# Another table of places for the last three graphs of a four-layer GNN stack

## The chip, the cores and the metric

The kernel runs on one core of a Trainium2 chip, in one launch. The metric is the device time of that launch in microseconds (us). Times of a kernel are given as the median of several runs; a profile is one execution of its own, with its own time.

## The reference

32 graphs of 512 nodes with 256 features (fp32) and a dense 512x512 integer adjacency each go, one by one and without any exchange, through four layers. Each layer is `h = relu(layernorm(x))`, `x = x + layer(h)`:

```python
x = x + _L0_gnn_ref(h, adj, W, a_src, a_dst)   # attention, 4 heads, additive scores, masked by adj > 0, elu
x = x + _L1_gnn_ref(h, adj, W, a)              # attention, 1 head, softmax over the other axis, elu
x = x + _L2_gnn_ref(h, adj, a_0, a_1, a_2, a_3)# scores (h*a_k) h^T, chosen by the value of adj, softmax
x = x + _L3_gnn_ref(h, adj, Wqkv, ..., W2, b2) # a transformer layer: 8 heads of 32, masked by
                                               # adj > 0 either way or the diagonal, layer norm,
                                               # feed-forward 256 -> 1024 -> 256, layer norm
```

All arithmetic is fp32.

## The kernel before

**How it is built.** `quick_path` does not issue instructions as it goes. A class `Plan` records *jobs*: one instruction of VectorE (DVE) or ScalarE (ACT), one DMA issue of SyncE (SP), or a few matmuls of TensorE (PE) that belong together. For each graph `b` the functions `masks`, `layer0`, `layer1`, `layer2` and `layer3` record 529 jobs, always the same ones, numbered by `plan.at` from 0 to 528. When all are recorded, `Plan.carry_out` sorts the jobs of all graphs by their *place*, issues them in that order, and ties each engine's instructions together, so that every engine, PE, DVE, ACT and SP alike, carries out its jobs strictly in the order of places. All jobs are issued from one line per kind: line 215 for DVE and ACT, 236 for SP, 266 and 268 for PE.

**What a place is.** Line 156:

```python
place = self.number * ROUND + self.own.get(self.number, self.table)[self.at] if self.place is None else self.place
```

`ROUND` is 100000. `PLACES` (line 291) holds one number for each of the 529 jobs of a graph, and all graphs use it but six: `OWN` (line 334) holds tables of their own for graphs 0, 1, 2, 29, 30 and 31. A place is a rank and nothing else: no instruction waits for a time. As the numbers of `PLACES` reach from 0 to some 459000 and graphs are 100000 apart, jobs of four to five graphs stand mixed in each engine's order: while PE does the feed-forward of one graph, DVE works on the attention of the next and ACT on the one behind. In the tables of graphs 29 to 31 the numbers reach into the millions: these only order the jobs at the end, where no further graph follows.

**Buffers.** `carry_out` also hands out buffers in the order of places: tiles of a kind share numbered slots (9 `big`, 19 `mid`, 8 `half`, 8 PSUM banks), a new tile gets the slot that has been free for longest, and its first writer waits for the last users of the tile before. So another order also gives other slots.

**The steps that the prediction names.** In `layer3`, the transformer layer:
- attention, for each of two groups `g` of four heads and four blocks `j` of 128 keys: a PE job `ps_s` (four score products, 32 rows deep), four ACT exponentials into `p`, one DVE product of `p` (128x2048) with the mask `m3`, a PE job `ps_ct` (four products with `v`), and from the second block on a DVE addition into `acc`, the sum that the softmax divides by. `acc` goes through a PE job `ps_to`, once for each group; the one of group 1 is the "second `ps_to`".
- the round trip of `inv`: ACT copies `ps_to` to `to`; SP sends it to DRAM and back (`to_d`, `seen`) so that it lies across partitions; DVE takes the reciprocals (`turned`); SP sends them out and back again (`in_d`, `inv`); DVE multiplies them into `cT`. Each step needs the one before.
- `ps_wo` (8 products of 256 columns) needs `cT` of both groups; DVE adds the residual (`t`), takes the norm's statistics (`st`, `mv`), ACT and DVE make `rstd` and `shift`, ACT writes four rows of `n`, PE transposes them (`ps_t3`; `ps_t` in the profile), ACT makes `tT`.
- the feed-forward: 16 products `ps_f1` of 512 columns, each pair followed by an ACT relu, then 32 products `ps_f2` of 256 columns; DVE adds them into `u`, the second norm gives `y`, and SP sends it out. The profile calls both `ps_f`.

In `layer1`, PE's `ps_sp` turns a small tile, and a DMA out and back spreads it into `rows1`, from which DVE makes the four blocks of `p1` that `ps_o1` needs; `layer2` has scores `ps_e`, transpositions `ps_y` and products `ps_o2`, both `ps_o` in the profile.

An fp32 product is two PE records in the profile, a transposition one.

## Time and profile before

| | us |
|---|---|
| median of 3 runs | 3430.3 |
| lowest and highest of them | 3425.57, 3436.63 |
| the profiled execution's own time | 3424.86 |
| its span, first to last instruction | 3422.9 |
| PE's mean granted clock, share of full speed | 0.994 |
| busy: PE, PE weight load, DVE, ACT | 3340.2, 1975.5, 2820.1, 2115.6 |
| PE's last product of the last graph ends | 3409.8 |

The page divides the span by engine, by 40 slices, by groups of equal instructions and by the chain of work that ended last. Lines name the source line, the engine, the operation and the tiles (output <- inputs, buffer numbers left out, so that `p` stands for `p0`, `p1`, `p2` and `p3`). As all jobs come from lines 215, 236, 266 and 268, tiles tell them apart, not lines. The view of waits gives total, number and longest wait for each pair of waiting and releasing instruction. The view of stages gives busy time of each engine within a window, with PE's granted clock there, the DMA engines' busy share and GB/s.

### The profile page before, as it was taken

The numbers are of one execution on the slowest core, as the hardware profiler recorded it, in microseconds if no ns is written. First come the engines' busy times: TensorE is split into PE (matmuls) and PEld (weight loads), VectorE is DVE, ScalarE is ACT, GpSimd is POOL, SyncE is SP. The second block draws the span as 40 slices with busy tenths as digits, with TensorE's granted clock in tenths as the row PEclk, the third lists the DMA queues.
The fourth block names the chain that finished last, engine by engine and source line by source line (L and its number), as shares of the span: only waits on it lengthen the run. The fifth ranks groups of instructions, "written<-read, shape, count | busy, mean of one in ns | idle before, by whom it ended". The sixth has DMA issues, their size and how long they took to land.

```text
span 3422.9 us, 48320 instructions
## 1 busy us (share of the span) xinstructions
PE 3340.2 (98%) x17842; PEld 1975.5 (58%) x17842; DVE 2820.1 (82%) x5499; ACT 2115.6 (62%) x4801; POOL 11.1 (0%) x25
## 2 busy tenths in 40 slices
PE   6999999999999999999999999999999999999995
PEld 4555566555566555665655665655655655655563
DVE  6887888888888888888888888888988888877954
ACT  5756667556666556676556676556676566675652
POOL 1000000000000000000000000000000000000000
PEclk9999999999999999999999999999999999999997
DMA  5111110111111111111111111111111111110000
GB/s 165 41 47 55 51 51 27 53 49 54 51 40 36 56 46 57 51 35 40 56 46 57 50 35 39 57 46 57 51 47 39 54 37 53 43 33 30 17 10 20
DMA packets 161171, 161.16 MB, mean 47 GB/s; under 512 B 92576, under 2 KB 126880, under 8 KB 156832
## 3 DMA queue, kind: packets, MB, share of 16 engines
q1 hardware_dynamic: 158464, 153.00, 15.3%
q0 software_dynamic: 1216, 3.94, 0.4%
q8 instruction: 143, 2.34, 0.3%
q10 hardware_dynamic: 1248, 1.05, 0.1%
q14 instruction: 100, 0.82, 0.1%
HBM read 122.96 MB, written 18.22 MB: 41 GB/s over the span
## 4 chain that ended last, share of the span: by engine, by line
PE 85%; DVE 8%; DMA 4%; ACT 3%; issue 1%; DVEq 0%; SPq 0%; ACTq 0%
PE ps_f L268 25%; PE ps_o L268 11%; PE ps_s L268 7%; PE ps_qk L268 6%; PE ps_wh L268 5%; PE ps_ct L268 5%; PE ps_oT L268 5%; PE ps_t L266 4%; PE ps_e L268 4%; PE ps_wo L268 3%; DVE p L215 3%; PE ps_v L268 3%; PE ps_den L268 3%; DMA inv<-in_d 2%; DVE acc L215 2%; PE ps_to L268 1%
## 5 line engine op out<-in xcount | busy, mean ns | idle before, releaser
L215 DVE TENSOR_TENSOR p<-p,m 128x2048 f32<-128x2048 f32 x256 | 577.8, 2277 | 3.3 <-ACT p L215 3.2
L215 ACT ACTIVATE p<-ps_s 128x512 f32<-128x512 f32 x1024 | 555.3, 616 | 35.0 <-PE ps_s L268 33.7
L268 PE MATMUL ps_f<-ff_t,f 128*128 128x256 f32 x2048 | 470.9, 381 | 0.0
L268 PE MATMUL ps_f<-tT,ff_t 128*128 128x512 f32 x1024 | 467.1, 597 | 0.4 <-ACT tT L215 0.4
L268 PEld LDWEIGHTS ps_f<-ff_t,f 128*128 128x128 f32 x2048 | 378.4, 190 | 87.7 <-issue 32.6
L215 DVE SCALAR_TENSOR_TENSOR p<-rows,seen,mT 128x512 f32<-128x512 f32 x512 | 352.7, 744 | 32.6 <-PE ps_oT L268 20.6
L215 ACT ACTIVATE rstd<-mv,eps 128x4 f32<-128x4 f32 x192 | 56.5, 294 | 522.4 <-DVE mv L215 509.5
L215 ACT ACTIVATE h<-x,shift,rstd 128x256 f32<-128x256 f32 x512 | 283.1, 599 | 94.5 <-DVE shift L215 94.2
L268 PEld LDWEIGHTS ps_f<-tT,ff_t 128*128 128x128 f32 x1024 | 185.4, 191 | 196.2 <-issue 154.5
L215 DVE TENSOR_TENSOR acc<-acc,p 128x2048 f32<-128x2048 f32 x128 | 292.5, 2285 | 2.3
L268 PE MATMUL ps_s<-qk 32*128 32x512 f32 x2048 | 287.9, 633 | 1.4 <-ACT qk L215 1.2
L215 ACT ACTIVATE f<-ps_f,ff1b_c 128x512 f32<-128x512 f32 x256 | 168.1, 684 | 132.3 <-PE ps_f L268 129.4
L268 PE MATMUL ps_ct<-p,v 128*32 128x512 f32 x2048 | 247.8, 599 | 0.0
L268 PE MATMUL ps_o<-h,p 128*128 128x257 f32 x1024 | 245.6, 383 | 0.5 <-DVE p L215 0.4
L268 PE MATMUL ps_o<-wh,p 128*128 128x256 f32 x1024 | 242.9, 385 | 0.4 <-ACT wh L215 0.4
L268 PE MATMUL ps_oT<-p,wh 128*32 128x512 f32 x2048 | 240.6, 594 | 0.0
L268 PE MATMUL ps_qk<-h3T,wqkv_t 128*128 128x512 f32 x512 | 239.2, 599 | 0.0
L268 PEld LDWEIGHTS ps_o<-wh,p 128*128 128x128 f32 x1024 | 189.9, 190 | 77.0 <-issue 25.9
L268 PEld LDWEIGHTS ps_o<-h,p 128*128 128x128 f32 x1024 | 189.1, 190 | 52.5 <-PE ps_den L268 20.1
L266 PE MATMUL ps_t<-ident,h 128*128 128x128 f32 x1024 | 171.7, 278 | 32.7 <-ACT h L215 31.9
L215 DVE BATCH_NORM_STATS2 st<-x 128x6 f32<-128x256 f32 x512 | 197.6, 413 | 5.7 <-DMA x<-in_x_dram 0.7
L266 PEld LDWEIGHTS ps_t<-ident,h 128*128 128x128 f32 x1024 | 127.5, 142 | 114.3 <-issue 71.0
(135 smaller groups left out, 4928.7 us busy)
## 6 DMA issues: line engine op xcount, KB each, us to landing
adj<-in_adj_dram SPq DMA_DIRECT2D x32, 1024.0 KB
rows<-rows_d SPq DMA_DIRECT2D x32, 1024.0 KB
x<-in_x_dram SPq DMA_DIRECT2D x32, 512.0 KB
rows<-rows_d SPq DMA_DIRECT2D x32, 512.0 KB
inv<-in_d SPq DMA_DIRECT2D x64, 256.0 KB
out_dram<-y SPq DMA_DIRECT2D x32, 512.0 KB
mT<-m SPq DMA_TRANSPOSE x128
ff_t<-in_L_gnn_W_dram POOLq DMA_DIRECT2D x2, 1024.0 KB, 10.3
```

The lines of the kernel that those rows point to most:

```text
L215: return [getattr(unit, method)(*map(real, args), **{k: real(v) for k, v in kw.items()})]
L266: made.append(self.nc.tensor.transpose(*map(real, c)))
L268: made.append(self.nc.tensor.matmul(*map(real, c[:3]), start=c[3], stop=c[4]))
```

## The change

The entries 29, 30 and 31 of `OWN` are replaced by other numbers, which come from a longer random search with another seed. `PLACES`, the tables of graphs 0 to 2, the jobs and everything else stay as they are; the new tables take three lines less, so later line numbers of the new kernel are lower by 3. The numbers themselves say little; the beginning of graph 29's entry and both ends of graph 31's, cut:

```diff
     29: [
-        -236579, 3207, 22971, 33312, 62191, 71856, 71856, 75652, 93034, 148594, 243484, 119139, 334671, 31308,
...
+        -189324, 11443, -5862, 99352, 68178, 68178, 68178, 92809, 223975, 322699, 231272, 289047, 254470, 15797,
...
     31: [
-        33325, -86294, 33325, 39506, 49469, 49469, 74208, 74208, 359509, 4777608, 899110, 1724524, 1803732, -86294,
...
+        9090606, 9090606, 9382868, 9404784, 9480495, 9476344, 9598301, 9617637, 9856870, 9938641, 9956511, 5774454,
+        5851003, 9419655,
     ],
```

Built, both kernels have the same 16,957 jobs. On PE 6216 jobs stand in order, and the two orders are equal up to job 5257; on DVE (5350) up to 4504, on ACT (4768) up to 4006, on SP (608) up to 469. GpSimd's 15 are equal. The last PE jobs of graph 30 and 31 before and after, by tile, with the number of jobs in a row:

```
before: 30:ps_f1 4  30:ps_f2 7  31:ps_t3 1  30:ps_f2 6  31:ps_t3 1  30:ps_f2 19  31:ps_t3 4  31:ps_qk 5  31:ps_s 1
        ... (31:ps_qk, ps_s, ps_v)  31:ps_ct 4  31:ps_s 1  31:ps_to 1  31:ps_s 1  31:ps_ct 1  31:ps_to 1  31:ps_ct 3
        31:ps_wo 8  31:ps_t3 8  31:ps_f1 14 ... 31:ps_f2 30
after:  31:ps_qk 4  31:ps_s 2 ... (31:ps_qk, ps_s, ps_v, ps_ct, 30:ps_t3)  31:ps_to 1  31:ps_s 1  30:ps_f1 8  30:ps_f2 1
        30:ps_f1 3  31:ps_ct 3  31:ps_to 1  31:ps_ct 1  30:ps_f1 3  30:ps_f2 3  30:ps_f1 1  30:ps_f2 1  30:ps_f1 1
        30:ps_f2 12  31:ps_wo 1  30:ps_f2 1  31:ps_wo 7  30:ps_f2 10  31:ps_t3 1 ... (30:ps_f2, 31:ps_t3)  31:ps_f1 11
        ... 31:ps_f2 25
```

(`ps_t3` here is the transposition of the norm named last, or of `h3` ahead of `ps_qk`.)

## The prediction

> **What bounds the kernel now.** I read the page first, then busy time by stage, TensorE's waits, and the chain of waits at the end.

> ```profile
> span 3422.9 us, 48320 instructions
> PE 3340.2 (98%) x17842; PEld 1975.5 (58%) x17842; DVE 2820.1 (82%) x5499; ACT 2115.6 (62%) x4801; POOL 11.1 (0%) x25
> ```

> TensorE (PE) is busy 98% of the span, and the change touches none of its instructions, only their order. So all there is to win or lose is PE's idle time and the time in which its clock is low. Where that lies, by stage (us, then busy PE, PEld, DVE, ACT, POOL, then PE's granted clock):

> ```profile
> 2839.50:3144.50 305.00, 303.10 (x1625) 178.41 (x1624) 252.86 (x479) 185.99 (x426) 0.00 (x0) 1.00 0.14 41
> 3144.50:3188.00 43.50, 42.46 (x236) 22.50 (x240) 42.69 (x50) 34.24 (x69) 0.00 (x0) 1.00 0.06 20
> 3188.00:3312.00 124.00, 122.13 (x567) 76.96 (x560) 81.76 (x169) 60.35 (x124) 0.00 (x0) 1.00 0.04 12
> 3342.60:3354.60 12.00, 0.00 (x0) 0.02 (x1) 11.77 (x7) 1.96 (x4) 0.00 (x0) 0.64 0.05 16
> 3354.60:3361.80 7.20, 7.14 (x36) 2.14 (x36) 1.89 (x4) 1.67 (x3) 0.00 (x0) 0.65 0.07 18
> 3361.80:3368.90 7.10, 0.03 (x1) 0.03 (x1) 2.47 (x5) 0.00 (x0) 0.00 (x0) 0.82 0.34 111
> 3368.90:3373.90 5.00, 4.97 (x12) 3.69 (x12) 1.46 (x4) 0.00 (x0) 0.00 (x0) 0.57 0.00 0
> 3377.60:3383.50 5.90, 5.12 (x12) 2.78 (x13) 3.19 (x3) 2.91 (x5) 0.00 (x0) 0.50 0.00 0
> ```

> Two things are to be seen. Up to 3342 PE hardly stops; after it, it stops three times and runs at a low clock behind each stop. And from 3144.5 to 3188.0 VectorE (DVE) is busy 42.69 of 43.50 us: that stretch, graph 29's attention, is DVE's. What PE waits for, from 2700 us on:

> ```profile
> PE ps_to L268 <- DVE acc L215: 12.1, 1, 12.1
> PE ps_wo L268 <- DVE cT L215: 7.1, 1, 7.1
> PE ps_t L266 <- ACT n L215: 4.1, 2, 3.8
> ```

> Single waits: graph 31's second softmax sum, its DMA round trip, its layer norm. The chain prices each link, and a full-clock batch of PE:

> ```profile
> 3334.82 3.57 PE ps_ct L268 x32
> 3338.39 1.07 PE ps_s L268 x8
> 3347.53 2.28 DVE acc L215
> 3356.60 0.58 ACT to L215
> 3360.60 0.25 DVE turned L215
> 3362.33 5.71 DMA inv<-in_d
> 3368.13 0.70 DVE cT L215
> ```

> Unit prices, start to start: a batch of four `ps_s` 1.07 us, of four `ps_ct` 0.88, of `ps_to` 0.86; a 512-wide product (`ps_f1`, `ps_qk`) 0.86, a 256-wide one (`ps_f2`, `ps_v`, `ps_wo`) 0.43, `ps_o` 1.74, a transposition 0.11. A 128x2048 `p` or `acc` on DVE takes 2.28 and starts 2.20 after the one ahead; an exponential on ScalarE (ACT) starts 0.48 after the last.

> **What the change moves.** Before and after hold the same 16,957 recorded jobs; the order of instructions differs on PE from its job 5257 (of 6216) on, some 570 us before PE's last product, on DVE and ACT a little later, and on SP from the same place. Nothing is added or removed, so the cost is in cover: the PE work that stands, in PE's order, between a result and the product that needs what is made of it. Counted from both orders with the unit prices, for the last three graphs, before -> after (us):
> - first `ps_s` to second `ps_to`: graph 29 39.0 -> 32.8, graph 30 42.7 -> 40.1, graph 31 19.9 -> 33.2
> - second `ps_to` to the first `ps_wo` that needs its `inv` (steady state 14.0): 11.0 -> 12.9, 14.9 -> 13.7, 4.4 -> 14.2
> - last `ps_wo` to the norm's first transposition: 19.6 -> 4.0, 10.3 -> 17.5, 0.4 -> 4.7 (of which 0.43 is that product)
> - `ps_sp` of layer 1 to its first `ps_o`: 21.8 -> 31.7, 47.1 -> 53.1, 22.3 -> 13.9

> In words: before, graph 30's feed-forward (27.5 us: 16 `ps_f1`, 32 `ps_f2`) ends ahead of graph 31's attention, which has PE to itself. After, 9.9 us of it stands inside that attention, 11.6 under the round trip of `inv`, 4.3 under the norm. In exchange graph 29's attention loses 6.2 us of cover.

> **Graph 29's attention.** From graph 28's `u` to graph 29's last `acc`, DVE carries the same instructions in both orders: 8 `p` and 6 `acc` at 2.20 (30.8), and 11.8 us of graphs 28 and 30; 42.6 together. PE's work up to the second `ps_to` is 39.4 us before and 33.3 after. Before, 42.6 by the sum came out as 43.0 in the trace (3144.5 to 3187.5). So DVE sets the end both times, PE stands still 9.3 us in sum where it stood 3.2, and arrives at about 3188 as before. It could be earlier than that by little, since DVE has no slack; it is later where DVE starves between (0 to 3 us), or where the low clock behind a stop reaches past DVE's end: a stop of 12 us was followed by 12.5 us at half clock, and PE's 12.6 us of work behind the first `ps_to` have 16.1 us of DVE's time to hide in; 12.5 us at half leave 6.3 undone, which ends 2.8 late. Bounds -1 and +6, value 0.

> **From there to PE's last product.** Before: 3187.7 to 3409.8, 222.1 us, for 181.9 us of PE work; 40.2 lost. Of these 23.7 are waits (12.1, 7.1, 4.1, 0.4), 7.2 the low clock (busy time times what the clock lacks: 7.14x0.35, 4.97x0.43, 5.12x0.50), and 9.3 small gaps, 5.2 of them in six of 0.4 to 1.6 us; the other 4.1 are 2.3% of the work. After, 188.0 us of work remain (the 6.1 that left graph 29's attention), with 2.3% (4.3), and with these exposed chains:
> - graph 29's `inv`: `ps_to` to `to` 1.1, to `turned` 4.0, to `cT` 7.2, `cT` 0.7, together 13.1 in its own row, against 12.9: 0.3 with the semaphore.
> - graph 29's norm: 3.8 from the last `ps_wo` to the first transposition (3373.87 to 3377.64), 1.5 more for the other three ACT rows, 0.8 for `tT`; cover 4.0, 0.9 in the transpositions: some 2.
> - graph 30's first sum 0.7, graph 31's layer 2 0.5: DVE's last `acc` and `p` against PE's place.
> - graph 31's attention: 1.07 for `ps_s`, 2.1 for exponentials, 14x2.20 on DVE, 0.2 for `turned`, 0.3 of semaphores = 34.6 against 33.2: 1.4, and 0.3 at its first sum.
> - its `inv` 13.1 to 14.2 against 14.2: 0.3; its norm 3.8 and `tT` 0.8 against 4.7 and what stands between the transpositions: 0.6.

> Sum 6.1; without any of them 0, at three times their size 18. SP's order moves too: the last three outputs are issued behind everything else, but graphs 29 and 30 have their `y` some 10 us ahead of graph 31's, so 0, at worst 5.3 (3417.6 to the end, one output) each. `rows1` of graph 31 needs 0.3, 5.9 and 5.4 on DVE, 0.6 on ACT: 12.2 against 13.9, so 0.

> **The sum.** 3187.7 + 188.0 + 4.3 + 6.1 = 3386.1 for PE's last product. The end behind it is unchanged: 3409.8 to 3422.9, 13.1. Span 3399.2; the execution's own time lies 2.0 above its span (3424.86), so 3401.2, 23.7 below. That execution is 5.4 below the median of the runs, 3430.3; against the median: 3407.

> **The rivals.**
> - *DVE's queue blocks on DMA* (the gain goes). From graph 29's to graph 31's second sum DVE has 109 us of work beside PE's 136.8. Four times `turned` and `cT` stand in DVE's order behind a DMA; where each is met too early, it stops DVE for up to 4.0 and 7.2: 44.8 us, DVE needs 153.8, PE ends 17 later: 3424. For it: both have little room in graph 31. Against: `cT` stands behind other work mostly. 8%.
> - *The clock* (slower). Six places have cover below or within 1 us of their chain: graph 29's sum, `inv` and norm, graph 30's sum, graph 31's sum and `inv`. If each stops PE long enough and brings 12.5 us at half clock with PE as the bound, each costs 6.2, together 37: 3444; it turns slower than before from the fourth. For it: all three stops at the end (12.1, 7.1, 3.8) were followed by a clock of 0.50. Against: the stretches to 3312 have gaps up to 1.6 and a clock of 1.00, and by my sum all but graph 29's first are 2 us or less. 4%. [...]
> - *Nothing exposed*: the listed chains fit their cover, and the small gaps of 4.3 are all that is lost: 3401. 15%.
> - *Graph 29's stretch runs on*: DVE starves and the clock adds, 7 later: 3414. 7%.
> - My forecast, 3407: 66%.

> **The numbers.** Range 3398 to 3420: exposures from 0 (3401) to 18 (3419), widened by 1 to 3 us for the runs' own scatter; it leaves out the 4% and the 8%, and some of the rest. 0.3% (10.3 us) is about what a measurement of this kernel can tell from no change. Faster: 66+15+7 = 88%; within it 8%, slower 4%.

> **What would show it.** Right: TensorE's idle time in the last 80 us gone but for some 5 us (the end behind the last product aside), the clock there near 1.00; graph 29's second `ps_to` at about 3188, behind waits for `acc` of 6 to 10 us; the last product near 3386. Wrong: that `ps_to` after 3194; new waits of over 3 us for `cT`, `n` or `acc` behind it; DVE idle on DMA in the last 190 us; a low clock beyond 3200.

## The result and the profile after

The changed kernel takes 3402.39 us, the median of 4 runs (3397.51 to 3405.7), against 3430.23 for the kernel before beside it: ratio 0.9916, interval 0.9896 to 0.9937. Two later pairs gave 0.9922 (0.9909 to 0.9935) and 0.9919 (0.9906 to 0.9932). The profiled execution took 3401.32, with a span of 3399.4. The page of after:

```profile
span 3399.4 us, 48314 instructions
PE 3337.5 (98%) x17842; PEld 1973.6 (58%) x17842; DVE 2823.3 (83%) x5499; ACT 2115.3 (62%) x4801; POOL 11.1 (0%) x25
```

Busy times are as before; what went is PE's idle time. By stage (us, then busy PE, PEld, DVE, ACT, POOL, then PE's granted clock):

```profile
3144.50:3188.00 43.50, 40.78 (x179) 22.12 (x179) 42.29 (x49) 28.92 (x58) 0.00 (x0) 0.92 0.06 19
3300.00:3340.00 40.00, 39.93 (x212) 16.50 (x205) 37.74 (x30) 27.73 (x53) 0.00 (x0) 1.00 0.03 8
3340.00:3386.00 46.00, 46.00 (x181) 33.11 (x180) 19.74 (x50) 14.85 (x30) 0.00 (x0) 1.00 0.08 29
```

By these rows PE stands still for 0.1 us in 86 from 3300 us to the last product, at full clock, where before it had three stops and a clock of 0.50 to 0.65 behind each. Its waits from 2700 us on (total, number, longest):

```profile
PE ps_n L1590 <- DVE least L1586: 3.7, 1, 3.7
PE ps_e L268 <- ACT ha L215: 1.3, 1, 1.3
PE ps_s L268 <- ACT qk L215: 0.8, 1, 0.8
PE ps_t L266 <- ACT n L215: 0.6, 3, 0.3
PE ps_to L268 <- DVE mv L215: 0.6, 1, 0.6
```

The waits of 12.1 for `acc` and 7.1 for `cT` are gone, and of the one of 3.8 for `n` at most 0.3 is left (`ps_n` stands behind the last graph). The chain of waits shows what lies in their place (start, length):

```profile
3321.36 10.07 PE ps_f L268 x24
3334.21 1.07 PE ps_to L268 x8
3336.13 11.40 PE ps_f L268 x42
3348.39 3.02 PE ps_wo L268 x14
3351.41 4.32 PE ps_f L268 x20
```

Graph 30's `ps_f` fill the time up to graph 31's second `ps_to`, then up to `ps_wo`, then behind it.

Single executions start their last stages several us apart: graph 28's last `ps_f2` starts at 3143.97 in the first profile of the changed kernel, at 3136.52 and 3139.76 in two more, with no difference in the order up to there. So I compare from that product on:

| us | from there to graph 29's second `ps_to` | on to the start of the last product | its end to the span's end |
|---|---|---|---|
| before | 43.84 | 221.51 | 13.1 |
| after | 45.21 | 196.27 | 13.3 |
| after, twice more | 44.49, 44.56 | 196.29, 196.29 | 13.3, 13.2 |

The change costs some 1 us in graph 29's attention and brings 25.2 behind it.

### The profile page after: what moved, and what is told of

Same layout as the page of the kernel before. It is cut to its first block, busy times and chain, and to the rows that moved or that the text cites. A ratio compares the mean times of both kernels' runs of the same rounds, so it can differ in the third digit from the quotient of the medians.

```text
span 3399.4 us, 48314 instructions
## 1 busy us (share of the span) xinstructions
PE 3337.5 (98%) x17842; PEld 1973.6 (58%) x17842; DVE 2823.3 (83%) x5499; ACT 2115.3 (62%) x4801; POOL 11.1 (0%) x25
## 4 chain that ended last, share of the span: by engine, by line
PE 81%; DVE 10%; DMA 6%; ACT 3%; issue 1%; SPq 0%; DVEq 0%; ACTq 0%
PE ps_f L268 26%; PE ps_o L268 10%; PE ps_s L268 6%; PE ps_qk L268 6%; PE ps_wh L268 5%; PE ps_ct L268 5%; PE ps_oT L268 5%; DVE p L215 4%; PE ps_t L266 4%; PE ps_e L268 3%; DMA inv<-in_d 3%; PE ps_wo L268 3%; DVE acc L215 3%; PE ps_v L268 2%; PE ps_den L268 2%; PE ps_to L268 1%
## 5 line engine op out<-in xcount | busy, mean ns | idle before, releaser
L215 DVE TENSOR_TENSOR p<-p,m 128x2048 f32<-128x2048 f32 x256 | 578.2, 2278 | 3.8 <-ACT p L215 3.6
L215 ACT ACTIVATE p<-ps_s 128x512 f32<-128x512 f32 x1024 | 554.8, 616 | 40.3 <-PE ps_s L268 36.4
L268 PE MATMUL ps_f<-ff_t,f 128*128 128x256 f32 x2048 | 471.2, 381 | 0.0
L268 PE MATMUL ps_f<-tT,ff_t 128*128 128x512 f32 x1024 | 466.6, 596 | 0.7 <-ACT tT L215 0.7
L268 PEld LDWEIGHTS ps_f<-ff_t,f 128*128 128x128 f32 x2048 | 379.1, 190 | 91.1 <-issue 36.6
L215 ACT ACTIVATE rstd<-mv,eps 128x4 f32<-128x4 f32 x192 | 56.5, 295 | 519.5 <-DVE mv L215 519.5
L215 DVE SCALAR_TENSOR_TENSOR p<-rows,seen,mT 128x512 f32<-128x512 f32 x512 | 352.6, 745 | 31.6 <-PE ps_oT L268 19.3
L215 ACT ACTIVATE h<-x,shift,rstd 128x256 f32<-128x256 f32 x512 | 282.8, 600 | 95.0 <-DVE shift L215 94.7
L268 PEld LDWEIGHTS ps_f<-tT,ff_t 128*128 128x128 f32 x1024 | 185.1, 190 | 194.5 <-issue 154.2
L215 DVE TENSOR_TENSOR acc<-acc,p 128x2048 f32<-128x2048 f32 x128 | 292.8, 2287 | 2.2
L268 PE MATMUL ps_s<-qk 32*128 32x512 f32 x2048 | 287.7, 633 | 1.3 <-ACT qk L215 1.1
L215 ACT ACTIVATE f<-ps_f,ff1b_c 128x512 f32<-128x512 f32 x256 | 168.8, 685 | 132.9 <-PE ps_f L268 125.9
L268 PE MATMUL ps_ct<-p,v 128*32 128x512 f32 x2048 | 245.4, 596 | 0.2 <-ACT v L215 0.2
L268 PE MATMUL ps_o<-h,p 128*128 128x257 f32 x1024 | 245.3, 383 | 0.0
L268 PE MATMUL ps_o<-wh,p 128*128 128x256 f32 x1024 | 242.8, 386 | 0.4 <-ACT wh L215 0.4
L268 PE MATMUL ps_qk<-h3T,wqkv_t 128*128 128x512 f32 x512 | 240.5, 600 | 0.0
L268 PE MATMUL ps_oT<-p,wh 128*32 128x512 f32 x2048 | 239.8, 594 | 0.0
L268 PEld LDWEIGHTS ps_o<-wh,p 128*128 128x128 f32 x1024 | 190.0, 190 | 78.2 <-issue 27.9
L268 PEld LDWEIGHTS ps_o<-h,p 128*128 128x128 f32 x1024 | 189.5, 190 | 51.5 <-PE ps_den L268 19.3
L215 DVE BATCH_NORM_STATS2 st<-x 128x6 f32<-128x256 f32 x512 | 197.3, 413 | 5.6 <-DMA x<-in_x_dram 0.4
L266 PE MATMUL ps_t<-ident,h 128*128 128x128 f32 x1024 | 170.0, 277 | 29.8 <-ACT h L215 29.5
L266 PEld LDWEIGHTS ps_t<-ident,h 128*128 128x128 f32 x1024 | 126.9, 141 | 112.3 <-issue 71.8
```

Source lines behind the costliest of these rows:

```text
L215: return [getattr(unit, method)(*map(real, args), **{k: real(v) for k, v in kw.items()})]
L266: made.append(self.nc.tensor.transpose(*map(real, c)))
L268: made.append(self.nc.tensor.matmul(*map(real, c[:3]), start=c[3], stop=c[4]))
```

## The experiments

**The theory**: the gain is the cover that graph 30's feed-forward gives graph 31's attention, `inv` and norm. Rival A: it was made ahead of 3300 us, by the new places of graphs 29 and 30. Rival B: stops share, so that taking one cover away costs little.

### Each cover taken away from the changed kernel

Only graph 30's feed-forward jobs get other places, just behind a job of graph 31; everything else stays. The edit of `no_cover_attention`, cut; the other three differ in jobs and place alone:

```diff
+for graph, places in {
+    30: {
+        447: 1666977.52, 448: 1666977.54, 449: 1666977.55, 450: 1666977.5, 451: 1666977.56, 452: 1666977.57,
...
+    },
+}.items():
+    OWN[graph] = list(OWN.get(graph, PLACES))
+    for at, place in places.items():
+        OWN[graph][at] = place
```

> The 9.9 us of graph 30's feed-forward (11 ps_f1, one ps_f2) that stand between graph 31's last ps_s and its second ps_to are put behind graph 31's last ps_ct; all other places stay. Theory (what the change brings is cover under graph 31's attention, inv and norm): PE meets the second ps_to 9.9 early, DVE's chain is the same, so PE waits 8 to 10 for p and acc there, and a low clock behind that stop costs 2 to 6 more: span 3411 to 3415 instead of 3399.4. Rival A (the gain was made ahead of 3300 us, in graphs 29 and 30): 3399 +-2. Rival B (a stop at one place shortens the later ones, since the moved products lie under inv next): under +6, at most 3405.

> The 11.6 us of graph 30's feed-forward (6 ps_f1, 16 ps_f2) that stand between graph 31's second ps_to and the end of its ps_wo are put behind graph 31's last ps_wo. Theory: PE waits for cT of both groups, 2.4 and 9.0, and a low clock adds 2 to 6: span 3411 to 3417 instead of 3399.4. Rival A (gain made ahead of 3300): 3399 +-2. Rival B (a stop shortens later ones; the norm has 11.6 more of cover): under +6, at most 3405.

> The 6.0 us of graph 30's ps_f2 (14) that stand from graph 31's last ps_wo on, ahead of and between the norm's transpositions, are put behind the last of these. Theory: PE waits 4.4 for n and 0.9 for tT, 0.8 in small pieces, and a low clock adds 0 to 4: span 3404 to 3409 instead of 3399.4. Rival A (gain made ahead of 3300): 3399 +-1. Rival B (the moved products hide tT and the relus behind): at most +2, 3401.

> All 48 feed-forward products of graph 30 that stand between graph 31's last ps_s and the norm's last transposition are put behind that transposition; graph 29's new places stay. Theory: the three stops add, 11.7 + 11.2 + 5.3 less what they share = 27.3, and 7 of low clock as before had it: span 3430 to 3436, that is 7 to 13 above the kernel before's 3422.9, since graph 29's attention keeps its smaller cover (6 of the 8.9 it lost were there). Rival A (gain made ahead of 3300): 3399 +-3. Rival B (stops share): 3410 to 3420.

| | ratio to before | span | from graph 29's second `ps_to` to the last product (after: 196.3) |
|---|---|---|---|
| `no_cover_attention` | 0.9965 (0.9951 to 0.9979) | 3418.1 | 209.5 |
| `no_cover_inv` | 0.9961 (0.9948 to 0.9974) | 3412.4 | 208.0 |
| `no_cover_norm` | 0.9954 (0.9938 to 0.9971) | 3410.6 | 207.0 |
| `no_cover_at_all` | 1.0011 (1.0001 to 1.0020) | 3436.4 | 227.5 |

PE's waits from 3290 us on in the first, the second, the third, and then with all cover gone:

```profile
PE ps_to L268 <- DVE acc L215: 8.1, 1, 8.1
```

```profile
PE ps_wo L268 <- DVE cT L215: 9.5, 2, 7.3
```

```profile
PE ps_t L266 <- ACT n L215: 4.0, 1, 4.0
```

```profile
PE ps_wo L268 <- DVE cT L215: 8.3, 2, 8.0
PE ps_to L268 <- DVE acc L215: 8.1, 1, 8.1
PE ps_t L266 <- ACT n L215: 3.9, 1, 3.9
```

Each stop comes where its cover was taken, at about the size expected: 8.1 for `acc` where 8 to 10 were expected for `p` and `acc`, 9.5 for `cT` where 2.4 and 9.0 were, 4.0 for `n` where 4.4 were. The costs are 13.2, 11.7 and 10.7; all together 31.2. Of the third, 1.7 lie in graph 29's norm, where the clock was low by chance (last section); without them the three add to 33.9. So the stops add almost fully, Rival B falls, and so does Rival A: with graph 29's and 30's other new places left as they are, the whole gain is gone. The sum also agrees with the kernel before. From graph 29's second `ps_to` to the end of the last product that kernel loses 40.2 us by the prediction's count (222.1 for 181.9 of PE's work), and `no_cover_at_all` loses 40.1 by the same count (228.1 for 188.0).

In `no_cover_attention` the clock was low for 10.2 us. It fell within the stop, and 5.9 us of it (3338.0 to 3343.9, clock 0.50) met PE's work: 2.9 lost, inside the 2 to 6 expected.

Three spans lie above their ranges. `no_cover_attention` is 3.1 above: its last stages start 3.9 later than after's (graph 28's last `ps_f2` at 3147.85), and the end behind the last product takes 1.8 longer. `no_cover_norm` is 1.6 above, by graph 29's norm, and `no_cover_at_all` 0.4, by where its last stages start (3150.39, 6.4 later than after's).

### One part alone, in the kernel before

> The kernel before with all its own places, except that 17.3 us of graph 30's feed-forward are put later: 7.8 (4 ps_f1, 10 ps_f2) behind the first of graph 31's four last ps_ct, 5.6 (13 ps_f2) behind the last of them, 3.9 (9 ps_f2) behind graph 31's last ps_wo; graph 30's second norm and output go behind graph 31's norm. Theory (cover at the end is the gain): the stops of 12.1, 7.1 and 4.1 shrink to some 4.7, 4.0 and 3.5, a new one of 1.9 comes at graph 31's h3, since its transpositions come earlier: 12 us less by the stops and 0 to 4 less low clock: span 3407 to 3411 instead of 3422.9, ratio to before 0.9955 +-0.001. Rival A (the gain was made by the new places of graphs 29 and 30): 3422.9 +-2, ratio 1.000. Rival B (the stop only moves to graph 31's h3): ratio 0.999 to 1.001.

```diff
+    30: {
+        468: 10724883.5, 469: 10724883.52, 470: 10724883.53, 465: 10724883.54, 466: 10724883.56, ...
+        478: 11071389.5, 479: 11071389.52, ... 481: 14303942.5, 482: 14303942.52, ... 505: 21401318.64, ...
```

Ratio 0.9960 (0.9948 to 0.9973), span 3410.4: as the theory said, and outside what either rival allows. PE's waits from 3180 us on:

```profile
PE ps_to L268 <- DVE acc L215: 4.3, 1, 4.3
PE ps_t L266 <- ACT n L215: 3.4, 2, 3.1
PE ps_t L266 <- ACT h L215: 3.2, 3, 1.7
PE ps_wo L268 <- DVE cT L215: 2.4, 1, 2.4
```

The third line holds the new stop at graph 31's `h3`, 1.7 where 1.9 was expected. Half of the gain comes with 17.3 of the 27.5 us, in the old order of everything else.

### What sets graph 29's attention

Three runs on one chip: the changed kernel again, with 3.5 us of DVE's work moved out of that stretch, and with 3.46 us more of PE's work in it.

> The changed kernel once more, as the base of the three runs beside it: ratio to before 0.9916 by its own runs, inside 0.9896 to 0.9937. From graph 28's last ps_f2 to graph 29's second ps_to 45.2 us +-1 (the low clock of 6.8 us in that stretch may fall elsewhere), from there to the last product's start 196.3 +-2.

> In the changed kernel three DVE instructions of graph 28 (x2 + b2 1.15, the two of y 1.16 each: 3.5 us) and its output DMA are put from the beginning of graph 29's attention to behind graph 30's shift, at about 3205 us, where DVE has time; nothing else moves. Theory (DVE's queue sets graph 29's stretch): 3.5 us leave the queue, and PE comes to the second ps_to earlier until the next chain sets it, ACT's ha for graph 30's ps_e: from graph 28's last ps_f2 to that ps_to 43.3 instead of 45.2, at least 41.7; the time 1 to 3 lower. Rival A (PE's own work and the low clock set the stretch): 45.2 +-0.4 and no change. Rival B (the moved work collides at 3205): ps_to earlier, and the time the same or higher.

```diff
+    28: {
+        406: 521301.5, 523: 521301.52, 524: 521301.54, 525: 521301.55,
+    },
```

> In the changed kernel four of graph 29's ps_v products are made three times over, the first two results being overwritten: 8 products of 0.43, 3.46 us of PE work more in graph 29's attention, and no other instruction. Theory (DVE sets the stretch and PE stands still 9 us in it): the stretch to the second ps_to grows by 0 to 1 (45.2 to 46.2), less if the fuller queue keeps the clock up. Rival A (PE is the bound, with its clock at half for 6.8 us): +3.5 or more, 48.7 and up, and the time +3.5.

```diff
-                    plan.matmuls(
-                        HALF,
+                    again = 2 if b == 29 and k == 0 else 0
+                    plan.matmuls(
+                        HALF * (1 + again),
+                        *((ps[:, i], hT[:, k, cut(2 * g + i, P)], wqkv_t[:, k, 2 * D : 3 * D], True, True),) * again,
                         (ps[:, i], hT[:, k, cut(2 * g + i, P)], wqkv_t[:, k, 2 * D : 3 * D], k == 0, k == KD - 1),
```

The stretch from graph 28's last `ps_f2` to graph 29's second `ps_to`, by stage, in the changed kernel, with less DVE work, and with more PE work:

```profile
3136.50:3181.00 44.50, 41.25 (x185) 22.12 (x183) 42.30 (x49) 30.40 (x61) 0.00 (x0) 0.96 0.06 19
```

```profile
3136.50:3178.90 42.40, 39.75 (x185) 21.78 (x184) 39.16 (x46) 30.22 (x61) 0.00 (x0) 1.00 0.02 7
```

```profile
3145.10:3190.60 45.50, 43.15 (x201) 24.83 (x199) 42.20 (x49) 30.24 (x61) 0.00 (x0) 1.00 0.06 18
```

DVE's busy time falls by 3.1 and the stretch by 2.1; PE's work grows by 3.46 and the stretch by 1.0. So PE is not the only bound (48.7 and up falls), and DVE's queue matters (45.2 +-0.4 falls). But the rows differ in the clock too: the first has 3.4 us at half clock, the other two none. Divided at graph 29's first `ps_to`, the stretch tells more:

| us | to the first `ps_to` | on to the second | of these at half clock | from DVE's last `acc` to the second `ps_to` |
|---|---|---|---|---|
| the changed kernel, three profiles | 27.64, 27.65, 27.65 | 17.6, 16.8, 16.9 | 4.8, 3.3, 3.4 | 1.4, 0.6, 0.9 |
| less DVE work | 26.46 | 15.9 | 0 | 0.6 |
| more PE work | 27.65 | 17.9 | 0 | 1.9 |

Up to the first `ps_to` DVE sets the time: the 0.86 us of added PE work that stand there cost nothing, and less DVE work brings 1.2. Behind it the two engines are nearly even. In the changed kernel DVE's last `acc` ends 16.0 to 16.2 us behind the first `ps_to`, and PE got to the second in 15.9 where its clock stayed high (less DVE work). So what comes on top for PE, a low clock or the other 2.6 us of added products, puts the second `ps_to` behind DVE's `acc`.

The time shows none of the 2.1: ratios 0.9922 (0.9909 to 0.9935), 0.9926 (0.9913 to 0.9938) and 0.9932 (0.9919 to 0.9945). The median with more PE work is 4.8 above the changed kernel's beside it, but their intervals overlap, and in the profiles 8.6 of 12.3 lie ahead of the stretch. With less DVE work, a new wait takes most of it back:

```profile
PE ps_qk L268 <- ACT h3T L215: 1.4, 1, 1.4
```

That is the collision of Rival B: the moved work stands ahead of DVE's `seen`, ACT's `wh` wait for `seen`, and in ACT's order graph 30's `h3T` stands behind them. The end behind the last product takes 1.2 longer as well (14.5 for 13.3).

### Can the order give more?

> Another order for the last 1348 jobs of graphs 28 to 31 in the changed kernel, worked out by stepping each engine's queue with the durations of this trace and keeping exchanges of neighbours that end earlier; it gives graph 28's last ps_f2 to graph 29's second ps_to 39.6 instead of 44.2, and graph 31's cover under attention, inv and norm as it is. Theory (queues in order, each instruction as long as in the trace, tell where PE stands): 9.3 us less than the changed kernel, 3390 +-3 for a span of 3399.4, the gain being ahead of 3200 us. Rival A (what is left in graph 29's stretch is the clock's and the hardware's, not the order's): 3399 +-2. Rival B (covers cut too fine): new stops over 1.5 us and a low clock, 3400 or more.

(The edit lists 1348 places.) The stretch was 39.56, as counted (39.6); the time was not: ratio 0.9919 (0.9906 to 0.9931), no different from the changed kernel, and the span of 3398.1 is within Rival A's 3399 +-2. Behind the stretch 202.9 us passed instead of 196.3, and the end took 16.2 instead of 13.3. One piece of that is seen among SP's waits from 3170 to 3200, with DVE's behind it (from 3170 to 3290) in the second fence:

```profile
SPq L236 <- DMA in_d<-turned: 4.9, 2, 3.8
```

```profile
DVE cT L215 <- DMA inv<-in_d: 5.0, 2, 2.9
```

This order lets DVE make graph 29's first `turned` only 1.4 us behind the second `ps_to` (10.7 ahead of it in the changed kernel). So two round trips run at once, and the second `in_d` took 4.3 us from its issue to the next DMA's issue, where it takes 1.5 alone. `cT` came 15.4 behind `ps_to` instead of 12.1, and PE waited 2.4, with 3.4 us at half clock behind it: what Rival B had named. The counting had priced each DMA by itself.

> As order_by_prices, from the changed kernel's order again, but an exchange is kept only by the mean of three countings: durations as in the trace, DMA 35% and DVE and ACT 3% longer, DMA 20% and ACT 8% longer; SP's jobs keep their places. By the trace's own durations it ends 6.2 earlier than the changed kernel. Theory (order_by_prices lost its gain because its covers had no room for longer transfers): 3 to 8 less than after_third beside it, no new stop over 2.5 us. Rival (what is left is not the order's to win): +-2 against after_third.

> The changed kernel once more, as the base of the two beside it: ratio to before 0.9916 to 0.9922, inside 0.990 to 0.994.

`order_with_room` has 0.9928 (0.9916 to 0.9941), the changed kernel beside it 0.9919 (0.9906 to 0.9932): no gain, as the rival has it, though by the medians (3399.65 and 3396.34) it is 3.3 longer and not within 2. No stop is over 2.5 us, but PE's last product came only 1.1 us sooner (409.9 against 411.0, from graph 29's first transposition in layer 1 on, which both orders share), and the end behind it took 17.3 us instead of 13.2. Its chain:

```profile
3384.97 1.23 DVE y L215
3386.20 0.19 DVE ok L215
3386.41 0.28 DVE least L1770
```

`least`, from which PE and DVE work out whether the general path must run, waits for one entry into `ok` that stands behind `y`; in the changed kernel it runs ahead of `y`.

> As order_with_room, with one DVE instruction placed otherwise: graph 30's last entry into ok (0.27 us), which stood behind the two DVE products of graph 31's y, goes behind those of graph 30's y. Theory (order_with_room came to PE's last product 1.1 us earlier than the changed kernel, and lost it since least, ps_n and the branch on it, some 9 us to the end, waited for that entry until y was done): from PE's last product to the end 13.2 instead of 17.3, as in the changed kernel; ratio to before 0.9915 instead of 0.9928. Rival (the end is the output DMA's): 17.3 as it was.

```diff
-        522: 173382, 523: 173393, 524: 173394, 525: 173398, 526: 173061, 527: 173436, 528: 173351,
+        522: 173382, 523: 173393, 524: 173394, 525: 173398, 526: 173061, 527: 173394.5, 528: 173351,
```

The end came to 14.4, not 13.2; ratio 0.9925 (0.9911 to 0.9938). The entry into `ok` was most of the longer end; the other 1.2 lie behind the last `y`, in its output. PE's last product came 411.4 behind the common point this time, 0.4 later than in the changed kernel, with a low clock of 3.4 us that `order_with_room` had not had. No version here beats the changed kernel by what can be measured. What else these orders lose against the counting (5 us in `order_with_room`) I have not traced to a cause.

## Why the prediction was right

**The mechanism.** The cover under graph 31's attention, `inv` and norm is the gain: shown by taking it away (all of the gain goes, in three stops at the three places) and by giving part of it to the kernel before (half of the gain).

**The sum.** Predicted for the profiled execution 3399.2 as a span, found 3399.4; the last product 3386.1, found 3386.05. That the total is right to 0.2 is luck, since two misses of 1.5 cancel in it:
- *Graph 29's second `ps_to` at 3187.7, value 0 of bounds -1 and +6*: it came at 3189.2. DVE's last `acc` ended at 3187.8, where the sum had it; the last 1.4 us were PE's, which had stood 1.5 for ACT's `ha` just before and had 3.6 us of `ps_e` to do. The two fences show DVE's last `acc` and PE's `ps_e` (start, length). The prediction had named such a case, a low clock that reaches past DVE's end, at 2.8, and put it at 0. Two further executions had 0.7 less.
- *From there 188.0 of work and 10.4 lost*: 8.9 lost. Graph 29's norm cost 2.0, as priced. Graph 31's layer 2 cost 0.33 for 0.5; a wait of 0.94 for `qk` was not in the sum. The other chains, 3.6 together (graph 30's first sum, graph 31's attention and norm, both `inv`), cost nothing that is visible: there the counted chains were too long. The small gaps are the rest, 5.6 for 4.3.
- *The end, 13.1*: 13.3.

```profile
3183.19 4.62 DVE L215 TENSOR_TENSOR acc<-acc,p 128x2048 f32<-128x2048 f32 x2
```

```profile
3185.54 3.71 PE ps_e L268 x10
```

**The form of graph 29's stops was wrong.** I had expected waits of 6 to 10 us for `acc`. There is none: PE's longest waits in the stretch are 1.3 for ACT's `ha` and, at the first `ps_to`, 0.6 for DVE. Of the some 12 us by which the stretch exceeds PE's work at unit prices, some 4 lie in `ps_s`, where the profile counts PE as busy. Four of these products took 1.07 us where they ran side by side (at 3308.8, for one); here their weight loads waited for ACT's exponentials, and from 3166.5 to 3169.0 four took 2.5. The wait of the weight loads:

```profile
PEld ps_s L268 <- ACT p L215: 2.4, 8, 0.8
```

And the low clock came there, as the page's stages show (the second is the window of the low clock):

```profile
3159.00:3169.60 10.60, 10.29 (x44) 4.34 (x38) 10.60 (x16) 7.62 (x15) 0.00 (x0) 1.00 0.06 18
3169.60:3176.40 6.80, 5.98 (x16) 2.63 (x17) 6.69 (x7) 4.66 (x11) 0.00 (x0) 0.50 0.01 2
```

It cost little because DVE was nearly the bound meanwhile: executions with 6.8, 3.4 and 3.4 us of it had 45.2, 44.5 and 44.6, and by the end of DVE's last `acc` alone it would have been some 44.

**The step from the profile to the median was mis-sized.** I added 5.4 because before's profile lay that far under its median, and got 3407; the profile after lies 1.1 under its median, 3402.39. The changed kernel's three profiles differ by 8.3 us in span, and 7.5 of these are there by graph 28's last `ps_f2`. So such a distance is the chance of one execution's earlier stages and no property of the kernel; for the kernel before there is one trace only.

**The rivals.** *DVE's queue blocks on DMA*: from 3180 us on DVE stood 4.5 us for `seen` and `inv` together, where the rival had 44.8. *The clock* needed four places of 6.2; one place, graph 29's attention, had a low clock, and its second `ps_to` came 1.4 behind DVE's `acc`. The 6.2 was too high by the trace of the kernel before: of the low clock at the first stop (13.65 us in the trace, where I had 12.5) 8.7 lay within the stop, from 3345.9 to 3354.6, and the work behind it lost 2.5 (7.14x0.35). At 2.5 each, six such places cost 15 and would not have used up the gain. *Graph 29's stretch runs on* had the sign right, at 1.4 for 7. *Nothing exposed*, 3401, lies nearer to the median than my 3407, but only by the 5.4 that was wrong: for the profiled execution it says 3395.1 and the forecast 3401.2, and it was 3401.3.

## What to carry to other kernels

Where every engine works through a list in order, count the PE work that stands between a result and its consumer and compare it with the chain between them: the counts found every stop of 4 us or more here, and the last unit of work, which has no successor to hide behind, is worth the most care. Spread the work ahead of it under its chains, and give each only what its chain needs, since cover in one place does nothing for the next. An order fitted to the microsecond by such counts, however, lost its counted 9 us, a part of it because two transfers that overlapped took longer than alone (4.3 us for 1.5). The order that left room for this did not win a measurable time either.

## What the runs showed of the hardware that I had not expected

I divided each trace from 150 us to the last product into pieces of this length, at these edges, and added up, in those at full clock, the time that the products' unit prices leave over. Of 13,056 pieces with less than 1.0 us left over the clock was halved in the next in none, of 151 with 1.0 to 1.95 in one, of 6 with 1.95 to 2.1 in two, of 23 with more in all. In the profile of the kernel before and the changed kernel's first alone, 1860 pieces had less than 1.0 and 24 had 1.0 to 1.8, none with a halved clock behind it; one had 2.05 (before, from 3199.15 us), without; and all five with 2.1 to 3.4 had it.

So in these traces a halved clock went with the sum in such a piece, some 2.0 us of 3.41, and not with one long stop. Nor need it be a stop: in the piece ahead of the low clock in graph 29's attention (3166.2 to 3169.6) 2.1 us were left over, of them 0.7 in stops and the rest in `ps_s` products that ran one or two at a time. Graph 29's norm, with 2.0 us in four stops of under 1 us, was followed by a low clock in two of the runs and cost 1.7 there (the `ps_f1` behind it took 8.0 us for 6.3), and by none where an edge divided it: in the changed kernel's first profile the edge lies at 3210.54, the pieces before and behind it had 1.0 and 1.4 left over, and the clock stayed at 1.00. This is one reason why the same order took up to 1.7 us more in one execution than in another.

My prediction held against the rival of the clock that most of the stops it counted would be 2 us or less. The trace of the kernel before did not show that such a stop is harmless: waits of up to 1.3 us from 2839 to 3312 us left the clock at 1.00, but one of 2.4 us, at 301 us, was followed by 3.41 us at half clock, and no single wait of PE from 150 us to 3312 us lies between these two.
